# Transposing layer 0's two normalised row tiles by VectorE block transposes and on-chip DMAs instead of TensorE

## The chip, the core and the metric

The kernel runs on one core of a Trainium2 chip. The metric is the device time of one execution in microseconds (us). Three runs of the kernel before gave 2903.96, 2904.14 and 2904.46 us; their median is 2904.14 us.

## The reference

64 independent graphs of 256 nodes with 256 features each go through two graph-attention layers. All arithmetic is 32-bit float.

```python
# layer 0, per graph (src: 256 x 256)
q, k = src @ Wq + bq, src @ Wk + bk                  # 8 heads of 32
attn = softmax(q @ k.T / sqrt(32))
out  = sum over r of (attn * (adj == r)) @ (src @ Wv[r] + bv[r])
x    = layernorm(src + out @ Wo + bo) * g1 + beta1
x    = layernorm(x + gelu(x @ W1 + b1) @ W2 + b2) * g2 + beta2
# layer 1, per graph
q, k, v = x @ Wq, x @ Wk, x @ Wv
e    = leaky_relu(q @ k.T, 0.2), edges with adj == 0 masked out
h    = layernorm(softmax(e) @ v)
y    = layernorm(concat(h, x) @ Wffn.T) + x
```

adj holds 0 and 1 alone, so only r = 0 and r = 1 of layer 0 matter.

## The kernel before, in words

One graph's activations fit in tiles of 128 partitions x 512 floats. "Rows" tiles hold nodes on the partitions (two blocks `t` of 128 nodes, 256 features each), "transposed" tiles hold features on the partitions (two blocks `c` of 128 features, 256 nodes each). A matmul contracts over partitions, so whatever is multiplied by a weight on its features must be in transposed form, while a layer norm, which sums over features, is done in rows form. So a normalised tile of layer 0 has to be transposed twice per graph: once after the first layer norm (`y0` to `y0T`, which feeds the matmuls `ph0`, `ph4`, `ph2`, `ph6` with W1, L665), and once after the second (`y1` to `y1T`, which feeds layer 1's `pq1`, `pk1`, `pv1` and `pwb`).

Each of the two goes like this in the kernel before (L653-654 and L692-693):

1. the rows tile with its residual added is in PSUM (`pwo` at L397, `pw2` at L397); VectorE takes the statistics (`mv0`, L406 to L410), GpSimd the reciprocal root (`rs0`, L415), VectorE writes the normalised rows `y0` to SBUF (L421, two instructions);
2. `transpose` (L364): TensorE transposes four 128x128 blocks of `y0` into the PSUM tile `py0` (L369);
3. `with_gain` (L380): ScalarE reads `py0`, applies gain and shift per feature (now per partition) and writes `y0T` (L385, two instructions).

`y0` is also read by GpSimd, which makes the residual for the next step from it (`r1`, and `x2` from `y1`).

PSUM tiles of the tag `g` (128 x 512 floats) come from four rotating buffers: a new `g` tile takes the buffer of the fourth `g` tile before it, and has to wait until that one's readers are done. `y` tiles have four buffers, `yT` tiles three, score tiles `s` two.

**The order of the work is written out by hand.** `program(g)` makes one graph's operations, each bound to one engine (PE = TensorE, ACT = ScalarE, DVE = VectorE, POOL = GpSimd, SP = the queue that issues DMAs). `in_order` (L45) sorts the operations of all graphs by `50 * graph + STARTS[name]`; every engine executes its own operations in that order, and semaphores between the engines keep the data dependencies. So the numbers of STARTS (L100) are places in a sequence, not times: the value modulo 50 is the place within one round of 50, and the whole part of value / 50 says how many rounds after the graph's own number it comes. One round holds one operation of each name, each for a different graph. The first four and the last four graphs have lists of their own (FIRST, L121, and LAST, L180). A name with `#2` is the second operation that writes this tile: `pwo` is the matmul, `pwo#2` VectorE's addition to it.

The operations around the change, with their engines: `pwo`, `pw2` ... `pw2#8` (PE, L357 and L683), `pwo#2`, `pw2#9` (DVE, L397), `mv0`, `mv1` (DVE), `rs0`, `rs1` (POOL), `y0`, `y1` (DVE), `py0`, `py1` (PE, L369), `y0T`, `y1T` (ACT, L385), then `ph0` ... `ph6` (PE, L665) and `pq1`, `pk1` (PE, L343), whose results ScalarE copies out as `q1`, `k1` (L513). On SP: the loads `xT`, `adj`, `x` (L334) of a later graph and the store `SP:y2` (L752) of an earlier one; four DMAs of 256 KB for each graph.

Of the kernel before, what the change touches and what calls it, by code (L numbers as in the profile page):

```python
# [9 lines left out]
F32 = mybir.dt.float32  # L10
I32 = mybir.dt.int32
AF = mybir.ActivationFunctionType
# [11 lines left out]
P = 128  # L24
D = 256
H, DH = 8, 32
KC = 2
NT = 2
# [16 lines left out]
def in_order(programs, starts, period, first, last):  # L45
# [4 lines left out]
    for g, p in enumerate(programs):  # L50
# [23 lines left out]
    "yT": ([KC, D], F32, 3),  # L74
    "hT": ([8, D], F32, 2),
# [25 lines left out]
    "xT": 47.54, "adj": 54.92, "neg": 55.74, "pq0": 56.97, "q0": 60.25, "pk0": 70.08, "k0": 70.90, "s000": 72.95,  # L101
    "e00/0": 81.15, "m00/1": 81.56, "m00/0": 87.70, "e00/1": 90.98, "pva0": 93.44, "s010": 94.26, "v0/0": 95.08,
    "e01/0": 96.72, "x": 97.13, "m00/1#2": 97.95, "pva1": 100.82, "res": 101.64, "e01/1": 102.05, "es00/1": 102.87,
    "v0/1": 103.28, "es01/0": 104.10, "m00/0#2": 106.56, "m01/1": 107.38, "m01/1#2": 107.79, "m01/0": 108.61,
    "m01/0#2": 109.43, "es00/0": 111.07, "po00": 111.48, "rd00": 112.30, "o0/0": 112.70, "es01/1": 113.11,
    "po01": 114.34, "rd01": 114.75, "o0/1": 115.16, "DVE:po01": 115.57, "DVE:po00": 116.39, "ACT:adj": 118.44,
    "pwo": 118.85, "pwo#2": 119.26, "mv0": 119.67, "rs0": 123.77, "y0": 124.18, "py0": 124.59, "y0T": 125.00,
    "r1": 129.51, "ph0": 131.97, "ph4": 132.79, "hT/0": 134.43, "hT/4": 134.84, "ph2": 135.25, "hT/2": 135.66,
    "ph6": 136.07, "hT/6": 136.48, "r1#2": 138.11, "pw2": 138.52, "pw2#2": 138.93, "pw2#3": 139.34, "pw2#4": 139.75,
    "pw2#5": 140.16, "pw2#6": 140.57, "pw2#7": 141.39, "pw2#8": 141.80, "pw2#9": 142.21, "mv1": 142.62,  # L110
    "rs1": 145.49, "y1": 145.90, "py1": 148.36, "y1T": 148.77, "pk1": 153.69, "pq1": 154.51, "k1": 155.33,
    "q1": 158.20, "s100": 159.02, "e10/0": 159.84, "m10/0": 160.66, "e10/1": 161.89, "x2": 163.52, "m10/1": 163.93,
    "s110": 165.98, "e11/0": 166.80, "m11/1": 167.21, "pv1": 167.62, "v1": 168.03, "m11/0": 170.49,
    "e10/1#2": 171.31, "e11/1": 172.13, "pwb": 172.54, "e10/0#2": 173.36, "e11/0#2": 175.41, "zb": 176.64,
    "e10/1#3": 177.05, "es10/1": 177.46, "e11/1#2": 182.38, "e10/0#3": 183.20, "e11/0#3": 183.61, "es10/0": 184.02,
    "e11/1#3": 186.89, "es11/1": 193.03, "po10": 193.85, "es11/0": 194.67, "po11": 196.31, "rd10": 199.18,
    "DVE:po11": 199.59, "o1/0": 200.00, "DVE:po10": 200.41, "rd11": 201.23, "o1/1": 202.46, "x2#2": 206.15,
    "ph": 221.72, "mv2": 225.82, "rs2": 226.23, "pwa": 227.87, "pwa#2": 228.28, "mv3": 228.69, "rs3": 229.10,
    "y2": 229.92, "y2#2": 230.33, "y2#3": 230.74, "SP:y2": 237.30,
# [3 lines left out]
        -6346.377, -6530.16, -6982.832, -6634.0, -6093.635, -5736.533, -6045.455, -6290.298, -5672.953, -5696.302,  # L123
        -5008.862, -5888.0, -6453.208, -5286.254, -5289.164, -5677.61, -5529.665, -5461.611, -5372.746, -5225.073,
        -6469.019, -6080.346, -6152.781, -6125.275, -4362.988, -5833.733, -5164.614, -4798.404, -4797.673, -4604.086,
        -4447.748, -4217.049, -4504.134, -4458.784, -4528.298, -4512.584, -4486.596, -4386.977, -4471.14, -4517.811,
        -4507.195, -4500.964, -4440.287, -4140.093, -3943.527, -3880.12, -4070.372, -4482.976, -4318.59, -4355.735,
        -3960.397, -4120.247, -4007.041, -4233.453, -3919.755, -3659.796, -3372.614, -3087.747, -3087.745, -3268.679,
        -2967.259, -2926.763, -2863.365, -2782.082, -2781.512, -2755.252, -2748.099, -2686.058, -2632.076, -2707.74,
        -2705.657, -2705.031, -2700.944, -2685.9, -2604.336, -2686.294, -2686.292, -2646.722, -2624.727, -2539.089,  # L130
        -2539.087, -2505.953, -2421.823, -2357.5, -2351.019, -2331.649, -2323.477, -2267.498, -2264.329, -2251.442,
        -2239.549, -2082.718, -1742.488, -2220.232, -2148.049, -2233.172, -2172.786, -1880.195, -1803.811, -1665.215,
        -1633.036, -2121.976, -2044.14, -1964.977, -1619.288, -1541.806, -1429.851, -2083.25, -1979.867, -1976.405,
        -1728.291, -1571.446, -1125.134, -1014.844, -994.266, -1059.277, -1945.625, -1773.239, -1843.378, -1724.266,
        -1604.233, -1188.745, -1683.584, -1843.165, -1482.837, -1349.351, -1250.224, -1002.469, -959.959, -933.061,
        -923.019, -780.327, -701.906, -611.768, -466.222, -464.592, -457.638, -381.397, -381.219, -245.27, -76.323,
        -60.729,
    ],
    [
        -3150.342, -2865.684, -3030.007, -2576.407, -1841.393, -2066.514, -2885.805, -2846.503, -2989.537, -2895.209,  # L140
        -2350.813, -2298.896, -2388.858, -2356.392, -2796.464, -2491.226, -2412.218, -2372.987, -2249.024, -2796.462,
        -2534.009, -2422.489, -2656.667, -2121.572, -1907.235, -1891.659, -1835.387, -2294.698, -2255.475, -2262.772,
        -2094.331, -2029.961, -2282.964, -2245.64, -2060.464, -2214.911, -2003.143, -1885.89, -1885.888, -1851.81,
        -1869.958, -1811.256, -1803.92, -1792.147, -1719.479, -1710.833, -1682.568, -1683.327, -1663.512, -1666.775,
        -1637.889, -1611.072, -1579.957, -1548.682, -1486.084, -1628.459, -1484.026, -1524.627, -1411.414, -1396.412,
        -1365.969, -1301.34, -1237.148, -1230.262, -1226.745, -1225.363, -1184.068, -1160.852, -1147.648, -1122.337,
        -1055.926, -668.081, -116.769, -1038.706, -1013.221, -1016.299, -997.935, -684.505, -533.528, -782.079,
        -585.735, -956.86, -945.562, -934.723, -729.07, -717.444, -487.763, -941.495, -932.268, -913.562, -765.459,
        -487.338, 86.712, 123.903, 138.251, 125.976, -832.305, -692.509, -819.769, -616.081, -456.587, -301.91,
        -623.652, -788.225, -329.295, -155.628, -127.412, 145.769, 188.646, 190.331, 169.782, 216.272, 226.254,  # L150
        229.932, 231.195, 236.668, 236.67, 238.046, 238.048, 267.639, 267.641, 273.454,
    ],
    [
        -2853.381, -1411.162, -2082.948, -1906.438, -455.655, -1016.668, -2267.454, -2048.524, -1765.164, -1744.282,
        -1234.866, -1230.669, -1174.61, -1071.551, -1744.28, -1452.623, -1459.483, -1353.241, -1089.619, -1529.289,
        -1443.514, -1245.603, -1125.376, -993.997, -951.211, -887.78, -955.455, -1234.076, -1105.384, -1194.403,
        -1071.068, -1064.103, -1157.836, -1089.956, -1017.329, -987.068, -974.658, -922.208, -875.651, -914.051,
        -833.048, -713.969, -707.805, -678.162, -644.192, -607.043, -606.639, -557.459, -429.974, -518.499, -481.768,
        -515.933, -464.185, -388.676, -273.434, -511.029, -416.896, -343.734, -251.228, -68.742, -31.021, -12.646,
        4.579, 4.581, 5.811, 5.813, 42.687, 42.689, 47.599, 68.12, 111.978, 136.328, 266.823, 118.18, 121.579,  # L160
        127.571, 145.419, 164.63, 167.189, 170.12, 182.669, 158.219, 158.221, 158.221, 160.93, 170.277, 192.81,
        158.272, 158.699, 167.979, 167.981, 184.986, 196.227, 197.919, 197.921, 196.229, 159.876, 168.344, 161.714,
        182.428, 182.43, 198.755, 171.609, 165.811, 174.875, 196.176, 196.908, 202.935, 209.414, 209.416, 202.937,
        222.627, 226.067, 227.191, 229.099, 229.955, 229.957, 229.959, 230.172, 242.113, 266.825, 267.746,
    ],
    [
        -1715.159, -307.399, -1860.875, -375.405, 68.756, 11.501, -1090.815, -1056.5, -890.959, -788.563, -40.809,
        -6.228, 12.243, 43.409, -699.157, -572.433, -263.057, 88.419, 14.512, -549.182, -172.795, -45.958, 0.679,
        108.906, 110.242, 113.133, 113.314, -14.853, -9.216, 103.608, 103.61, 70.071, 22.889, 13.277, 66.318, 95.567,
        109.714, 115.504, 115.506, 113.587, 119.215, 122.548, 122.55, 122.552, 127.137, 129.396, 129.398, 138.847,  # L170
# [66 lines left out]
def fast_path(nc, tc, a, out, bad):  # L237
# [13 lines left out]
    with ExitStack() as ctx:  # L251
# [63 lines left out]
        def program(g):  # L315
            ops, used = [], {}

            def T(name):
                return at_(g, name)
# [755 lines left out]
```

## Time and profile before

| | |
|---|---|
| time, median of three runs | 2904.14 us |
| time of the profiled execution | 2903.45 us |
| span of its profile | 2901.5 us |
| TensorE (PE) busy | 2863.8 us, 99% |
| GpSimd (POOL) busy | 2008.1 us, 69% |
| VectorE (DVE) busy | 1964.0 us, 68% |
| ScalarE (ACT) busy | 1776.7 us, 61% |
| DMA queue of SP | 7.9% of the 16 DMA engines' time |
| `py` transposes on PE (L369) | 512, 84.8 us busy in total |
| gain and shift on ACT (L385) | 256, 130.4 us busy in total |

The profile is one execution. "Busy" is the time in which at least one instruction of an engine was under way; matmuls are pipelined, so the duration of one is longer than the distance to the next. "SPq" is the instruction queue of SP, and its DMA rows give the time that the issue took, not the transfer. The chain of waits follows the work that ended last back through whatever released each step. The timeline lists the instructions of an engine in order of time: start, duration, what it is, how many of the same kind follow each other.

### The profile page before, as it was taken

What the parts mean: (1) busy time and instruction counts of PE and PEld (TensorE: products, weight loads), DVE (VectorE), ACT (ScalarE), POOL (GpSimd) and SP (SyncE); (2) the same over time, 40 slices, a digit from 0 to 9 for tenths busy, and PEclk for the clock granted to TensorE, in tenths of its full rate; (3) what the DMA queues carried; (4) which work ended last, traced back from release to release, by engine and by line L of the source; (5) the groups of instructions that cost most, each with busy time, mean ns of one, the idle gap of its engine ahead of it and who ended that gap; (6) DMA issues with size and microseconds to landing.
All of it is one profiled execution on the core that took longest, in us unless ns stands there. A gap on an engine that the chain in (4) does not pass through costs nothing.

```text
span 2901.5 us, 53555 instructions
## 1 busy us (share of the span) xinstructions
PE 2863.8 (99%) x21770; PEld 2152.2 (74%) x21770; DVE 1964.0 (68%) x3668; ACT 1776.7 (61%) x3011; POOL 2008.1 (69%) x1542
## 2 busy tenths in 40 slices
PE   7999999999999999999999999999999999999996
PEld 5777777777777777777777777777777777777775
DVE  4676676766766767667667666676676676766765
ACT  4656656666666566566665665666666656666563
POOL 2667667677677676776776766767767667677666
PEclk9999999999999999999999999999999999999998
DMA  3000000000000000000000000000000000011000
GB/s 113 24 29 19 28 17 30 16 30 30 16 30 30 16 30 15 30 30 16 30 30 16 30 22 23 30 16 30 30 15 30 30 16 30 15 34 34 8 23 12
DMA packets 74331, 76.63 MB, mean 26 GB/s; under 512 B 4449, under 2 KB 73569, under 8 KB 74081
## 3 DMA queue, kind: packets, MB, share of 16 engines
q1 hardware_dynamic: 74080, 73.17, 7.9%
q8 instruction: 173, 2.83, 0.4%
q14 instruction: 78, 0.63, 0.1%
HBM read 56.37 MB, written 16.78 MB: 25 GB/s over the span
## 4 chain that ended last, share of the span: by engine, by line
PE 97%; DVE 1%; POOL 1%; issue 1%; DMA 0%; ACT 0%; SPq 0%; DVEq 0%; POOLq 0%
PE ph L665 15%; PE pw L683 15%; PE po L477 12%; PE s L439 9%; PE pq L343 8%; PE pk L343 8%; PE pva L617 7%; PE pv L357 4%; PE pwa L357 4%; PE pwo L357 4%; PE po L482 4%; PE pwb L357 4%; PE py L369 3%; PE ph L369 1%; POOL e L717 0%
## 5 line engine op out<-in xcount | busy, mean ns | idle before, releaser
L717 POOL TENSOR_TENSOR e<-e,m 128x1024 f32<-128x1024 f32 x256 | 600.3, 2354 | 301.5 <-ACT m L713 299.5
L508 POOL TENSOR_TENSOR es<-e 128x512 f32<-128x512 f32 x512 | 647.1, 1275 | 168.2 <-ACT e L455 127.4
L455 ACT ACTIVATE e<-s 128x1024 f32<-128x1024 f32 x256 | 260.1, 1016 | 389.0 <-PE s L439 363.2
L665 PE MATMUL ph<-y0T,w 128*128 128x256 f32 x2048 | 452.9, 379 | 0.0
L683 PE MATMUL pw<-w,hT 128*128 128x256 f32 x2048 | 452.7, 379 | 0.0
L491 DVE RECIPROCAL rd<-po 128x256 f32<-128x256 f32 x256 | 448.4, 1752 | 2.9 <-PE po L482 2.9
L415 POOL TENSOR_TENSOR rs<-ve,neg_half 128x2 f32<-128x2 f32 x256 | 179.2, 700 | 386.0 <-DVE ve L410 380.8
L665 PEld LDWEIGHTS ph<-y0T,w 128*128 128x128 f32 x2048 | 389.0, 190 | 53.4 <-issue 0.7
L683 PEld LDWEIGHTS pw<-w,hT 128*128 128x128 f32 x2048 | 389.2, 190 | 52.8
L464 DVE TENSOR_TENSOR e<-s,neg 128x1024 f32<-128x1024 f32 x256 | 305.9, 1216 | 155.6 <-PE s L439 152.5
L713 ACT ACTIVATE m<-s 128x1024 f32<-128x1024 f32 x256 | 260.9, 1021 | 228.5 <-PE s L439 140.7
L397 DVE TENSOR_TENSOR pw<-pw,r 128x512 f32<-128x512 f32 x64 | 44.8, 700 | 471.8 <-PE pw L683 464.3
L464 DVE TENSOR_TENSOR m<-s,neg 128x1024 f32<-128x1024 f32 x256 | 301.0, 1213 | 37.4 <-ACT e L455 23.5
L439 PE MATMUL s<-q,k 32*128 32x256 f32 x4096 | 294.2, 400 | 1.9 <-DVE m L464 1.1
L477 PE MATMUL po<-e,v 128*32 128x256 f32 x4096 | 275.3, 385 | 6.1 <-ACT v L513 4.0
L455 ACT ACTIVATE e<-e 128x1024 f32<-128x1024 f32 x256 | 268.8, 1054 | 19.9 <-POOL e L717 19.6
L455 ACT ACTIVATE m<-m 128x1024 f32<-128x1024 f32 x256 | 264.0, 1055 | 9.1 <-DVE m L464 9.0
L439 PEld LDWEIGHTS s<-q,k 32*128 32x128 f32 x4096 | 185.4, 184 | 105.6 <-issue 48.1
L617 PE MATMUL pva<-wv,xT 128*128 128x512 f32 x512 | 241.1, 593 | 0.0
L477 PEld LDWEIGHTS po<-e,v 128*32 128x32 f32 x4096 | 114.9, 110 | 148.3 <-issue 84.6
L672 ACT ACTIVATE hT<-ph,cols 128x256 f32<-128x256 f32 x512 | 196.2, 478 | 11.0 <-PE ph L665 10.2
L385 ACT ACTIVATE y0T<-py,cols 128x256 f32<-128x256 f32 x128 | 65.2, 559 | 182.4 <-PE py L369 182.3
(90 smaller groups left out, 4688.3 us busy)
## 6 DMA issues: line engine op xcount, KB each, us to landing
xT<-xT_dram SPq DMA_DIRECT2D x64, 256.0 KB, 3.0
adj<-adjT_dram SPq DMA_DIRECT2D x64, 256.0 KB, 3.6
x<-x_dram SPq DMA_DIRECT2D x64, 256.0 KB, 2.8
out_dram<-y SPq DMA_DIRECT2D x64, 256.0 KB, 2.2
w<-L_gnn_W_dram SPq DMA_DIRECT2D x2, 1024.0 KB, 10.1
rows<-rows_dram SPq DMA_DIRECT2D x1, 896.0 KB, 8.2
wv<-L_gnn_Wv_dram SPq DMA_DIRECT2D x3, 256.0 KB, 3.2
wk<-L_gnn_Wk_dram SPq DMA_DIRECT2D x2, 256.0 KB, 6.9
```

The source lines that it names most:

```text
L343: nc.tensor.matmul(pt[:, o, :], lhsT=w[:, c, o * P : (o + 1) * P], rhs=s[:, c, :], start=(c == 0), stop=(c == KC - 1),)
L357: nc.tensor.matmul(pt[:, t, :], lhsT=T(s)[:, c, t * P : (t + 1) * P], rhs=w, start=(n == 0), stop=(n == len(parts) - 1),)
L439: nc.tensor.matmul(s[j // 2][:, j % 2, c, :], lhsT=kT[r, hg, c * P : (c + 1) * P], rhs=qT[r, hg, :], start=True, stop=True,)
L455: nc.scalar.activation(T(dst)[:, j], s, AF.Exp, scale=scale, **kw)
L464: lambda: nc.vector.tensor_tensor(T(dst)[:, j], T(src), T("neg")[:, None].to_broadcast([P, 2, NT, D]), ALU.add),
L477: nc.tensor.matmul(po[j * DH : (j + 1) * DH, 0, :], lhsT=v(c, j), rhs=T(e)[:, j, c, :], start=(n == 0 and c == 0), stop=(n == len(parts) - ...
L491: op("DVE", [po], [f"{rd}:rd"], lambda: nc.vector.reciprocal(T(rd), T(po)[:, 1, :]))
L508: lambda: on.tensor_tensor(T(dst)[:, j], T(e)[:, j, 0, :], T(e)[:, j, 1, :], ALU.add),
L617: nc.tensor.matmul(pv.rearrange("p r d -> p (r d)"), lhsT=s[:, c, t * P : (t + 1) * P], rhs=wv0[:, c].rearrange("p r d -> p (r d)"), start ...
L665: nc.tensor.matmul(ph[:, i, :], lhsT=w1[:, c, (f + i) * P : (f + i + 1) * P], rhs=s[:, c, :], start=(c == 0), stop=(c == KC - 1),)
L683: nc.tensor.matmul(T("pw2")[:, t, :], lhsT=T("hT")[:, f + i, t * P : (t + 1) * P], rhs=w2[:, f + i, :], start=(f + i == 0), stop=(f + i == ...
L717: nc.gpsimd.tensor_tensor(T(f"e1{hg}")[:, j], T(f"e1{hg}")[:, j], T(f"m1{hg}")[:, j], ALU.add)
```

## The change

`transpose` is no longer called for `y0` and `y1`, and the PSUM tiles `py0` and `py1` are gone. In their place `turned` does the transposition in two operations: one VectorE instruction transposes every 32x32 block of the rows tile within its own 32 partitions and writes the result to a new SBUF tile `y0b` (tag `yb`, two buffers), and 16 DMAs on SP, each of 16 KB in runs of 128 bytes, bring the blocks to the partitions where they belong in `y0T`. ScalarE then applies gain and shift to `y0T` in place, reading SBUF instead of PSUM. The order of the operations is a new one in all three tables.

```diff
 TAGS:
     "yT": ([KC, D], F32, 3),
+    "yb": ([KC, NT, P], F32, 2),
...
+            def turned(src, dst):
+                blocks = f"{src}b"
+                def emit_blocks():
+                    nc.vector.transpose(
+                        out=T(blocks), in_=T(src).rearrange("p t (c f) -> p c t f", c=KC)
+                    )
+                def emit_places():
+                    for a in range(4):
+                        for b in range(4):
+                            nc.sync.dma_start(
+                                out=T(dst)[32 * b : 32 * b + 32].rearrange("p c (t n) -> p c t n", t=NT)[
+                                    :, :, :, 32 * a : 32 * a + 32
+                                ],
+                                in_=T(blocks)[32 * a : 32 * a + 32, :, :, 32 * b : 32 * b + 32],
+                            )
+                op("DVE", [src], [f"{blocks}:yb"], emit_blocks)
+                op("SP", [blocks], [f"{dst}:yT"], emit_places)
-            def with_gain(src, dst, gain, shift):
+            def with_gain(name, gain, shift):
...
-                            T(name)[:, c, :], T(src)[:, c, :], AF.Identity,
+                            T(name)[:, c, :], T(name)[:, c, :], AF.Identity,
...
-            transpose("y0", "py0")
-            with_gain("py0", "y0T:yT", g10c, be10c)
+            turned("y0", "y0T")
+            with_gain("y0T", g10c, be10c)
...
-            transpose("y1", "py1")
-            with_gain("py1", "y1T:yT", g20c, be20c)
+            turned("y1", "y1T")
+            with_gain("y1T", g20c, be20c)
```

The new STARTS (FIRST and LAST are replaced by new lists of the same kind). `y0T` and `y1T` are now the 16 DMAs on SP, `y0T#2` and `y1T#2` ScalarE's gain and shift:

```diff
+    "xT": 30.24, "adj": 35.48, "pk0": 35.89, "k0": 36.29, "x": 40.32, "neg": 40.73, "pq0": 41.13, "q0": 43.15,
+    "s010": 43.55, "e01/0": 44.35, "pva0": 45.16, "m01/1": 45.56, "v0/0": 45.97, "e01/1": 46.77, "m01/0": 47.98,
+    "pva1": 48.39, "v0/1": 49.19, "s000": 52.02, "m01/1#2": 52.42, "res": 53.23, "e00/1": 54.03, "m00/0": 56.85,
+    "es00/1": 57.66, "m00/0#2": 58.47, "e00/0": 58.87, "es01/0": 59.68, "m00/1": 62.10, "m00/1#2": 63.71,
+    "m01/0#2": 65.73, "es00/0": 66.13, "po00": 67.34, "es01/1": 70.16, "po01": 70.56, "rd01": 70.97, "rd00": 72.58,
+    "DVE:po01": 72.98, "DVE:po00": 73.79, "o0/0": 76.21, "o0/1": 79.84, "pwo": 86.69, "pwo#2": 87.50, "mv0": 87.90,
+    "rs0": 89.52, "y0": 89.92, "y0b": 93.95, "r1": 100.81, "y0T": 103.63, "y0T#2": 105.24, "ACT:adj": 109.27,
+    "r1#2": 112.50, "ph0": 112.90, "ph4": 113.31, "ph2": 116.53, "hT/2": 118.15, "hT/0": 118.55, "hT/4": 121.37,
+    "ph6": 124.60, "hT/6": 125.00, "pw2": 127.02, "pw2#2": 127.82, "pw2#3": 128.23, "pw2#4": 128.63,
+    "pw2#5": 130.65, "pw2#6": 131.05, "pw2#7": 131.45, "pw2#8": 131.85, "pw2#9": 132.26, "mv1": 132.66,
+    "rs1": 133.87, "y1": 134.27, "y1b": 137.10, "y1T": 144.76, "y1T#2": 147.18, "pq1": 152.82, "pk1": 156.05,
+    "k1": 157.26, "q1": 158.06, "x2": 160.08, "s110": 166.94, "e11/1": 167.74, "e11/0": 168.95, "m11/1": 169.35,
+    "m11/0": 169.76, "e11/1#2": 172.18, "s100": 173.39, "e10/0": 174.19, "e11/1#3": 175.81, "e10/1": 176.61,
+    "m10/0": 179.03, "e10/0#2": 179.44, "m10/1": 183.06, "e10/1#2": 183.47, "e10/1#3": 184.68, "e11/0#2": 185.08,
+    "pwb": 188.31, "e10/0#3": 188.71, "zb": 189.11, "es10/1": 191.53, "pv1": 192.34, "e11/0#3": 192.74,
+    "v1": 196.37, "es10/0": 197.58, "es11/0": 198.79, "po10": 199.60, "es11/1": 200.00, "po11": 200.40,
+    "rd10": 201.21, "DVE:po11": 201.61, "rd11": 204.44, "o1/0": 204.84, "DVE:po10": 205.65, "o1/1": 206.45,
+    "ph": 210.48, "pwa": 210.89, "mv2": 211.29, "rs2": 211.69, "pwa#2": 214.11, "mv3": 214.52, "rs3": 214.92,
+    "y2": 215.32, "x2#2": 221.77, "y2#2": 225.40, "y2#3": 227.42, "SP:y2": 241.94,
```

Sorted modulo 50, TensorE's round in the order before is `pva1 pk1 pq1 pq0 s100 po00 po01 s110 pv1 pwo pk0 ph pwb s000 py0 pwa ph0 ph4 ph2 ph6 pw2 ... pw2#8 pva0 po10 s010 po11 py1`, and SP's is `adj SP:y2 x xT`. TensorE's round in the new order is `po11 s000 pq1 pk1 ph pwa ph0 ph4 ph2 s110 po00 po01 s100 ph6 pw2 ... pw2#8 pk0 pwo pwb pq0 pv1 s010 pva0 pva1 po10`, and SP's round is `y0T xT adj x SP:y2 y1T`.

## Prediction

> **What bounds the kernel now.** I read the head of the page first, then the busy times of one stretch in the middle, then TensorE's timeline in that stretch.
>
> ```profile
> span 2901.5 us, 53555 instructions
> PE 2863.8 (99%) x21770; PEld 2152.2 (74%) x21770; DVE 1964.0 (68%) x3668; ACT 1776.7 (61%) x3011; POOL 2008.1 (69%) x1542
> ```
>
> ```profile
> 1000.00:1044.50 44.50, 44.50 (x342) 33.52 (x341) 30.56 (x58) 27.64 (x48) 31.39 (x25) 1.00 0.08 25
> ```
>
> The second line covers one round: window, length, then busy time of PE, PE's weight loads, DVE, ACT, POOL, then the granted clock (1.00). SP's stores come 44.5 us apart, so one graph takes 44.5 us, and PE is busy in all of it. No other engine is busy for more than 31.4 us. TensorE's work is the limit in the middle, and what leaves it shortens the round, unless something else then ends last.
>
> ```profile
> 1015.87 1.15 PE L439 MATMUL s<-q,k 32*128 32x256 f32 x16
> 1016.95 0.66 PE L369 MATMUL py<-ident,y 128*128 128x128 f32 x4
> 1017.44 1.89 PE L357 MATMUL pwa<-wf,o 128*128 128x256 f32 x8
> ...
> 1032.98 1.88 PE L617 MATMUL pva<-wv,xT 128*128 128x512 f32 x4
> ...
> 1038.73 0.66 PE L369 MATMUL py<-ident,y 128*128 128x128 f32 x4
> 1039.22 0.59 PE L617 MATMUL pva<-wv,xT 128*128 128x512 f32 x1
> ```
>
> Read the starts, not the durations: the work behind a `py` starts 0.49 us after it (1017.44 - 1016.95, 1039.22 - 1038.73). That is a `py`'s price on PE.
>
> **Removed.** Two `py` a graph, 0.98 us, times 64: 62.7 us off PE. (The Trainium skill, "TensorE: Matmul & The Clock Gate", Part 4, gives about 275 ns for a transpose in a kernel's context. The duration in the trace agrees, a median of 273 ns, but four follow each other within 0.49 us, so 512 x 275 ns = 141 us would overstate the gain.) The round would fall to 44.5 - 0.98 = 43.5 us. Two PSUM tiles of tag `g` per graph go as well; PE waits for nothing in the round now, so that gains nothing.
>
> **Added on DVE.** 128 block transposes of 128x512 floats; the trace has none. Nearest row: an addition of that shape, 0.68 to 0.70 us (L397). The ends are 0.41 us (a 128x256 operation, L494) and 3.5 us (twice the reciprocal's 1.75 us for 128x256). I take 0.68: DVE goes from 30.6 to 31.9 us a round and stays hidden behind PE, except in the latency below.
>
> **Changed on ACT.** The gain reads SBUF instead of PSUM. ACT's exponentials of 128x1024 take 1054 ns from SBUF and 1016 ns from PSUM, so at 4% more it is nothing on an engine that is 62% busy.
>
> **Added on SP: 32 DMAs a graph**, beside the four there are. What matters is the distance between two issues.
>
> ```profile
> 0.73 0.40 SPq L520 DMA_DIRECT2D cols<-cols_dram  x1
> 1.18 0.42 SPq L520 DMA_DIRECT2D wv<-L_gnn_Wv_dram  x1
> ```
>
> ```profile
> 1026.30 0.38 SPq L752 DMA_DIRECT2D out_dram<-y  x1
> 1026.73 0.46 SPq L334 DMA_DIRECT2D x<-x_dram  x1
> 1027.28 0.46 SPq L334 DMA_DIRECT2D xT<-xT_dram  x1
> 1027.83 0.42 SPq L334 DMA_DIRECT2D adj<-adjT_dram  x1
> ```
>
> `cols` is the only one of like size (12 KB in 128 runs): the next begins 0.45 us later. After the 256 KB store it is 0.43, between the 256 KB loads 0.55. The shortest issue is 0.37 us, so 0.42 with a gap of 0.05. I take **0.45**, from the nearest row; the ends are 0.42 and 0.55. Time to landing:
>
> ```profile
> out_dram<-y SPq DMA_DIRECT2D x64, 256.0 KB, 2.2
> cols<-cols_dram SPq DMA_DIRECT2D x1, 12.0 KB, 1.7
> ```
>
> I take 1.7 us for 16 KB; 2.2 is the other end. SP's busy time, 36 x 0.45 = 16 us of 43.5, is no limit, and 34 MB more (128 x 256 KB) in short runs, beside today's 73, falls on DMA engines that are 7.9% busy. The transfers of the loads are ordered before their use by a whole stretch of the round, so the loads that are now queued behind 16 or 32 issues still come in time. (A rule that speaks against the change: the Trainium skill, "DMA: Bandwidth & Descriptors", Rules for kernel authors, wants small transfers joined, since under 64 KB one pays mostly overhead, and puts the fixed part of one DMA near 2 us. If it were paid one after the other, 32 x 2 = 64 us a graph would make the kernel over 4000 us; the trace shows issues 0.45 us apart and landings of 1.7 us, so the fixed part overlaps.)
>
> **The added wait, and what it must fit into.** A `py` was ready half a microsecond after `y`; now there are 16 DMAs between. In the new order, between the end of a graph's `pw2#8` and the next `ph0` (of the following graph), PE has, by the starts in the timeline: `pk0 pwo pwb pq0 pq1 pk1 pwa`, 7 x 1.73; `pv1` 1.82; `s010` and `s000`, 2 x 1.08; `pva0` 1.72; `pva1` 1.81; `po10` 1.32; `po11` 1.43; `ph` 0.44. Together **22.8 us** of cover. The other 20.6 us, from `ph0` to `pw2#8`, make up the round.
>
> Against it stands a chain, because SP's order puts both transpositions one behind the other: `y1T` (place 44.76 of a round; its data hangs on `pw2#8`), then at once `y0T` of the following graph (place 3.63 of the next round), which `ph0` needs. How long VectorE's part takes can be read at the end of the chain of waits, where nothing else is in its way:
>
> ```profile
> 2854.01 0.71 DVE pw L397
> ...
> 2854.74 0.76 DVE st L406 x2
> 2855.50 0.22 DVE mv L408 x2
> 2855.72 0.20 DVE ve L410 x2
> ...
> 2855.98 0.71 POOL rs L415
> ...
> 2856.72 1.01 DVE y L421 x2
> ```
>
> From `pw` to the end of `y`: 3.72 us. The chain: 0.30 until VectorE sees `pw2#8` (PE's next work starts at 1032.98, VectorE at 1033.28); 3.72; 0.3, an estimate, for `rs1` behind a 2.35 us addition of `e` on POOL; 0.68 for `y1b`; 0.3, an estimate, for hand-overs and buffer waits: SP starts at 5.3 us. The 32nd issue starts 31 x 0.45 = 13.95 later, at 19.25, and has landed at 20.95 (`y0b` is ready near 10, long before SP reaches it). ACT: gain 1.02 (two instructions in the timeline), then `k1` and `q1`, 1.07, which the order queues behind the gain and which `ph0` needs, since its PSUM buffer is the one of `pq1`, four `g` tiles earlier. Hand-over 0.1: **23.15 us against 22.8**. `ph0` comes 0.34 us late in each round, 63 x 0.34 = 21 us. (`y1T` alone lands at 13.8, gain until 14.9; `pq1` has 17.2 us of cover: hidden.)
>
> **Start and end.** In the last 40 us PE is idle a good part of the time (14.58 of 20 us busy, then 6.98 of 21.5), and the chain runs through `py` and gain of the last graph's `y1`: 1.2 us there become 0.68 + 15 x 0.45 + 1.7 + 1.0 = 10.1. One such exposure, about 8 us; the other three at the two ends (first graph's, last graph's `y0`) I take as covered by other graphs' scores.
>
> **Sum**, against the profiled execution's own 2903.45 us (span 2901.5; 0.7 below the median of 2904.14): 2903.45 - 62.7 + 21 + 8 = 2869.8; **2870 us**.
>
> **Rivals.**
>
> 1. *All hidden.* At 0.42 us an issue the chain is 22.2 us and fits; the wait of 21 us is gone: 2849 us. With a covered end, 2841. For it: three issues in the trace at 0.37 to 0.38. Together with the forecast's own neighbourhood (up to 2885) 0.50; between there and 2898 us another 0.07.
> 2. *Slower, by SP's issue distance.* Each 0.01 us per issue costs 31 x 0.01 x 63 = 20 us once the chain is longer than its cover. From 0.467 us on the whole gain is lost; at the loads' 0.55 the chain is 26.25, 3.44 us over in each round, 217 us: 2903.45 - 62.7 + 217 + 8 = 3066 us. Halfway, at 0.50, 2968. Against it: those rows move 256 KB each, 16 times as much, and each of the later ones stands behind another. For it: the break-even is only 0.02 us off, and a landing of 2.2 us would add 32 us more. 0.37, of which up to 3010 us 0.22, beyond 0.15; into the latter fall a block transpose at the upper end (2.8 us more in the chain, 178 us: 3048) and DMAs that wait for each other to land: 32 x 1.7 = 54 us is longer than a round, 64 x 54 = some 3500 us.
> 3. *It does not take work off the limit*: wait and gain cancel, within 0.2% (about what a measurement of this kernel can tell from no change), 2898 to 2910: 0.06.
>
> Range: 2838 (all hidden, a `py` slot 0.05 larger) to 3010, which leaves out about 0.17. The likeliest case's own range is 2840 to 2890. Faster 0.57, same 0.06, slower 0.37.
>
> **What would show it.** In the profile after: no `py` on PE; the round between SP's stores 43.5 us if hidden, 43.9 as forecast, 46.9 in the slow case; a gap on PE ahead of `ph0` put down to ACT (`q1` or the gain), and ACT's gain waiting for a DMA; 16 issues on SP 0.45 us apart. I am wrong if PE is as full as before and yet the round isn't shorter, if the gap on PE is ahead of `pq1`, or if the issues wait for landings.

## The result, and the profile after

The changed kernel takes **3392.35 us** (median of four runs, 3387.91 to 3397.56); beside it on the same chip the kernel before took 2904.30 us. The ratio is 1.1681, 95% interval 1.1661 to 1.1701: 488 us slower, where 34 us faster was forecast. The profiled execution took 3387.91 us, span 3386.1 us.

The head of the page after (busy time, share of the span, instructions), and the chain of waits by engine:

```profile
span 3386.1 us, 56035 instructions
PE 2964.1 (88%) x21258; PEld 2190.3 (65%) x21258; DVE 2041.6 (60%) x3796; ACT 1789.9 (53%) x3011; POOL 2007.2 (59%) x1542
PE 60%; SPq 28%; DMA 4%; issue 3%; ACT 2%; DVE 1%; POOL 1%; ACTq 0%; DVEq 0%; POOLq 0%
```

The 512 `py` matmuls are gone (21770 to 21258), yet PE's busy time has risen by 100 us and its share fallen from 99% to 88%. SP's queue, which computes nothing, now holds 28% of the chain that ended last; by line all of it is L394, the 32 DMAs of a graph. PE both stands idle and works slower. The timelines of one round show where. SP first (start, duration, what, how many in a row):

```profile
1409.75 0.38 SPq L774 DMA_DIRECT2D out_dram<-y  x1
1421.33 10.74 SPq L394 DMA_DIRECT2D y1T<-y1b  x16
1432.19 10.97 SPq L394 DMA_DIRECT2D y0T<-y0b  x16
1443.20 0.59 SPq L336 DMA_DIRECT2D xT<-xT_dram  x1
```

Each burst of 16 takes almost 11 us, and `y0T` starts where `y1T` ends. ACT's two gains in the same round (in brackets: idle time ahead, and what ended it), then PE around them:

```profile
1434.55 1.09 ACT L407 ACTIVATE y1T<-y1T,cols 128x256 f32<-128x256 f32 x2 [5.49 <-DMA y0T<-y0b]
...
1444.87 1.09 ACT L407 ACTIVATE y0T<-y0T,cols 128x256 f32<-128x256 f32 x2 [7.29 <-DMA y0T<-y0b]
1445.87 0.56 ACT L535 COPY k<-pk 128x512 f32<-128x512 f32 x1
```

```profile
1435.20 2.05 PE L345 MATMUL pq<-y1T,wq 128*128 128x256 f32 x8 [1.35 <-DMA y0T<-y0b]
...
1439.26 1.89 PE L359 MATMUL pwa<-wf,o 128*128 128x256 f32 x8
1446.48 8.38 PE L687 MATMUL ph<-y0T,w 128*128 128x256 f32 x24 [5.34 <-ACT k L535]
1454.79 1.15 PE L461 MATMUL s<-q,k 32*128 32x256 f32 x16
```

(The brackets at 1434.55 and 1435.20 name `y0T`, but by the trace `y1T`'s last DMA landed at 1434.29 and `y0T`'s first at 1434.74, behind the gain's start: what the gain of `y1T` waited for, and `pq1` behind it, is `y1T`.) PE has nothing to do for 5.34 us ahead of `ph0`: ACT waits for the DMA, makes the gain, copies `k1`, and only then may `ph0` start. And the 24 `ph` matmuls behind the gap take 8.31 us until the next start (1454.79 - 1446.48), where 24 of them took 5.27 in rounds without a gap. The stretches of that round, with window, length, busy PE, PEld, DVE, ACT, POOL, granted clock, DMA share and GB/s, say why:

```profile
1416.55:1439.26 22.71, 21.36 (x150) 15.20 (x149) 17.04 (x32) 10.55 (x20) 15.63 (x13) 1.00 0.13 18
1439.26:1446.48 7.22, 1.89 (x10) 1.33 (x8) 5.45 (x17) 1.61 (x4) 4.71 (x5) 0.94 0.25 56
1446.48:1449.00 2.52, 2.52 (x6) 2.07 (x7) 0.00 (x0) 2.52 (x5) 0.05 (x1) 0.50 0.00 0
1449.00:1452.00 3.00, 3.00 (x8) 2.37 (x8) 0.00 (x0) 2.98 (x5) 3.00 (x3) 0.50 0.45 107
1452.00:1455.00 3.00, 3.00 (x16) 2.35 (x19) 0.00 (x0) 0.87 (x2) 0.67 (x1) 0.93 0.19 68
```

Behind the gap the granted clock (the share of TensorE's full clock) is 0.50 for 5.9 us: the 5.52 us up to 1452.00 and, by the mean of 0.93 in the last stretch, 0.4 more. Half of 5.9 us is 2.95, nearly all of the 3.04 us by which these 24 matmuls take longer. (The Trainium skill, "TensorE: Matmul & The Clock Gate", Part 1, says that an idle window of about 3.4 us brings the clock to 4/8. The 0.50 behind a gap of 5.34 us agrees.) PE is "busy" in those stretches: that is why its busy time rose.

So one round, 44.5 us before, is 52.0 us now (mean distance of SP's stores over 41 rounds, 50.8 to 53.6). Means over 48 rounds give its parts: 43.5 of work, 5.4 of gap ahead of `ph0`, 0.6 ahead of `pq1`, 2.2 of slow clock in `ph` (7.5 instead of 5.34 busy); 0.3 is left over. 60 rounds of 7.5 us more are 450 of the 484 us between the two profiled executions; of the other 34, 8.5 lie ahead of SP's first store (150.5 us from the start, 142.0 before), the rest among the first and the last graphs; I did not follow them further.

### The profile page after: what moved, and what is told of

Its sections match the earlier page's. It is cut to its first block, busy times and chain, and to the rows that moved or that the text cites. A ratio compares the mean times of both kernels' runs of the same rounds, so it can differ in the third digit from the quotient of the medians.

```text
span 3386.1 us, 56035 instructions
## 1 busy us (share of the span) xinstructions
PE 2964.1 (88%) x21258; PEld 2190.3 (65%) x21258; DVE 2041.6 (60%) x3796; ACT 1789.9 (53%) x3011; POOL 2007.2 (59%) x1542
## 4 chain that ended last, share of the span: by engine, by line
PE 60%; SPq 28%; DMA 4%; issue 3%; ACT 2%; DVE 1%; POOL 1%; ACTq 0%; DVEq 0%; POOLq 0%
SPq L394 28%; PE ph L687 17%; PE pw L705 13%; PE po L499 8%; PE s L461 5%; PE pk L345 3%; PE pwo L359 3%; PE pwb L359 3%; PE pva L639 3%; PE po L504 2%; DMA y0T<-y0b 2%; DMA xT<-xT_dram 2%; PE pq L345 2%; PE pv L359 1%; ACT y0T L407 1%
## 5 line engine op out<-in xcount | busy, mean ns | idle before, releaser
L530 POOL TENSOR_TENSOR es<-e 128x512 f32<-128x512 f32 x512 | 638.1, 1271 | 562.4 <-ACT e L477 554.6
L687 PE MATMUL ph<-y0T,w 128*128 128x256 f32 x2048 | 592.8, 454 | 319.9 <-ACT k L535 172.6
L687 PEld LDWEIGHTS ph<-y0T,w 128*128 128x128 f32 x2048 | 462.5, 232 | 446.8 <-ACT k L535 314.3
L513 DVE RECIPROCAL rd<-po 128x256 f32<-128x256 f32 x256 | 440.6, 1739 | 179.8 <-PE po L504 179.7
L486 DVE TENSOR_TENSOR m<-s,neg 128x1024 f32<-128x1024 f32 x256 | 311.0, 1217 | 92.4 <-PE s L461 70.2
L694 ACT ACTIVATE hT<-ph,cols 128x256 f32<-128x256 f32 x512 | 206.9, 473 | 264.4 <-PE ph L687 264.3
L407 ACT ACTIVATE y0T<-y0T,cols 128x256 f32<-128x256 f32 x128 | 69.8, 592 | 444.8 <-DMA y0T<-y0b 444.8
L407 ACT ACTIVATE y1T<-y1T,cols 128x256 f32<-128x256 f32 x128 | 69.9, 593 | 309.9 <-DMA y1T<-y1b 277.3
```

Source lines behind the costliest of these rows:

```text
L486: lambda: nc.vector.tensor_tensor(T(dst)[:, j], T(src), T("neg")[:, None].to_broadcast([P, 2, NT, D]), ALU.add),
L513: op("DVE", [po], [f"{rd}:rd"], lambda: nc.vector.reciprocal(T(rd), T(po)[:, 1, :]))
L530: lambda: on.tensor_tensor(T(dst)[:, j], T(e)[:, j, 0, :], T(e)[:, j, 1, :], ALU.add),
L687: nc.tensor.matmul(ph[:, i, :], lhsT=w1[:, c, (f + i) * P : (f + i + 1) * P], rhs=s[:, c, :], start=(c == 0), stop=(c == KC - 1),)
```

## The experiments

**Is it the transposition's latency or the new order?** `order_only` keeps the new order and puts both transpositions back on TensorE.

```diff
-            turned("y0", "y0T")
-            with_gain("y0T", g10c, be10c)
+            turned_pe("y0", "y0T")                    # 4 PE transposes into PSUM
+            with_gain_pe("y0b", "y0T", g10c, be10c)   # gain from PSUM, as before
     (the same for y1; "y1b" moved from 137.10 to 139.50)
```

> The changed kernel with both transpositions back on TensorE (gain read from PSUM again), in the new order; y1's transposition stands two places later on TensorE than VectorE's one did. Theory (SP's issue distance, 0.65 us a DMA, makes ph0 late): nothing is left on SP, TensorE is full again, 44.5 us a round, 2900 to 2930 us. Rival (the new order itself, e.g. k1 and q1 queued behind the gain, costs the time): a gap ahead of ph0 stays and the time is above 3150 us.

Measured 2974.51 us (2968.14 to 2978.78), ratio 1.0240 [1.0223, 1.0257]. PE in `order_only`:

```profile
1443.24 1.89 PE L359 MATMUL pwa<-wf,o 128*128 128x256 f32 x8
1444.96 5.34 PE L709 MATMUL ph<-y0T,w 128*128 128x256 f32 x24
```

Rounds of 44.9 us, no gap ahead of `ph0`. The order alone costs some 70 us, more than I expected, only 24 us (60 x 0.4) of it in the middle, the rest among the first and the last graphs. The other 418 us come with the DMAs.

**Is it the number of DMAs?** `eight` halves it. Which 32x32 block goes where is left out (the blocks stay in their partitions), so only its time counts.

```diff
-                    for a in range(4):
+                    for a in range(2):
                         for b in range(4):
...
-                                    :, :, :, 32 * a : 32 * a + 32
+                                    :, :, :, 64 * a : 64 * a + 64
...
-                                in_=T(blocks)[32 * a : 32 * a + 32, :, :, 32 * b : 32 * b + 32],
+                                in_=T(blocks)[32 * b : 32 * b + 32, :, :, 64 * a : 64 * a + 64],
```

> 8 DMAs of 32 KB in runs of 256 bytes in place of 16 of 16 KB; the blocks stay in their own 32 partitions, so the exchange of blocks between partition groups is left out. Bytes are the same. Theory (number of issues times 0.65 us): the chain is 4.8 + 15 x 0.66 + 2.1 + 1.9 = 18.7 us against 22.8 of cover, no gap ahead of ph0, round 43.5 us, 2845 to 2870 us. Rival (bytes or landing times on the DMA engines): 3300 to 3400 us.

Measured 2867.04 us (2862.96 to 2868.05), ratio 0.9872 [0.9855, 0.9888], as expected. The SP and PE timelines of `eight`:

```profile
1417.29 5.11 SPq L394 DMA_DIRECT2D y1T<-y1b  x8
1422.51 6.04 SPq L394 DMA_DIRECT2D y0T<-y0b  x8
```

```profile
1433.73 1.89 PE L359 MATMUL pwa<-wf,o 128*128 128x256 f32 x8
1435.46 5.34 PE L687 MATMUL ph<-y0T,w 128*128 128x256 f32 x24
```

Twice the bytes in half as many DMAs, and one issue costs the same. The bursts halve, `ph0` follows `pwa` without a gap, the round is 43.6 us: just what the removal of the `py` promised. The same volume does no harm, and neither does VectorE's part.

**One transposition of the two.** `y0_dma` does only `y0` by blocks and DMAs, `y1_dma` only `y1`; the other is on TensorE as in `order_only`.

```diff
 y0_dma:
-            turned("y1", "y1T")
-            with_gain("y1T", g20c, be20c)
+            turned_pe("y1", "y1T")
+            with_gain_pe("y1b", "y1T", g20c, be20c)
     (y1_dma: the same for y0)
```

> Only y0 goes by block transposes and DMAs; y1 is transposed on TensorE again (two places later than its block transpose stood), in the new order. Theory (the two transpositions queue on SP, each 16 x 0.66 = 10.6 us): y0b is ready 9.1 us after pw2#8, its DMAs are through at 9.1 + 15 x 0.66 + 2.1 = 21.1, gain and k1 until 23.0, against 22.8 + 0.5 of cover: hidden, round 44.0 to 44.5 us, 2900 to 2960 us with the ends as in order_only. Rival (each transposition by itself costs half of the loss, by its landing or its place in the order): 3130 to 3200 us.

> Only y1 goes by block transposes and DMAs; y0 is transposed on TensorE again, in the new order. Theory: y1T's DMAs start 4.8 us after pw2#8, are through at 4.8 + 15 x 0.66 + 2.1 = 16.8, gain until 18.1, against 17.2 + 0.5 of cover ahead of pq1: 0.4 us late at most, round 44.0 to 44.9 us, 2890 to 2960 us. Rival (each transposition by itself costs half of the loss): 3130 to 3200 us.

Measured 2934.66 us (ratio 1.0102 [1.0085, 1.0119], rounds 44.0) and 2953.31 us (1.0172 [1.0155, 1.0189], rounds 44.5). Neither has a gap ahead of `ph0` (`y1_dma` has 0.4 us a round ahead of `pq1` and `pk1`). Both times lie in the ranges expected. Each is even some 20 to 40 us faster than `order_only`; it takes both in one chain to lose 418 us.

**What makes an issue take 0.60 us?** `plain` moves runs of 512 bytes instead of 128, `wide16` uses all 128 partitions in each of the 16 DMAs (and also loads `x` in four quarters, to see DMAs of other kinds behind each other). Both leave out the right places of the blocks.

```diff
 plain:
-                                out=T(dst)[32 * b : 32 * b + 32].rearrange("p c (t n) -> p c t n", t=NT)[
-                                    :, :, :, 32 * a : 32 * a + 32
-                                ],
-                                in_=T(blocks)[32 * a : 32 * a + 32, :, :, 32 * b : 32 * b + 32],
+                                out=T(dst)[32 * b : 32 * b + 32].rearrange("p c (t n) -> p (c t) n", t=NT)[:, a],
+                                in_=T(blocks)[32 * a : 32 * a + 32].rearrange("p c t n -> p (c t) n")[:, b],
 wide16:
...
+                    for j in range(16):
+                        nc.sync.dma_start(
+                            out=T(dst).rearrange("p c n -> p (c n)")[:, 32 * j : 32 * j + 32],
+                            in_=T(blocks).rearrange("p c t n -> p (c t n)")[:, 32 * j : 32 * j + 32],
+                        )
...
+                for b in range(4):
+                    nc.sync.dma_start(out=T("x")[32 * b : 32 * b + 32], in_=ap[32 * b : 32 * b + 32])
```

> 16 DMAs of 16 KB between groups of 32 partitions as in the change, but each moves one run of 512 bytes per partition in place of four of 128; the places within a row are left out, so the transposed tile is in a wrong order. If the 0.60 us of an issue come from the pattern (four short runs a partition, 128 descriptors): issue 0.37 to 0.45, chain 4.8 + 31 x 0.45 + 2.1 + 1.9 = 22.7, 2845 to 2900 us. If they come from a DMA between two partition groups of SBUF whatever its runs: issue 0.60, 3390 us.

> 16 DMAs of 16 KB within SBUF per transposition as in the change, but each over all 128 partitions (one run of 128 bytes a partition, same partition to same partition; the exchange of blocks is left out), and the load of x from HBM split into four DMAs of 32 partitions. It measures the issue: if SBUF to SBUF makes it 0.6 us, y0T and y1T stay at 0.60 and the x loads at 0.37 to 0.46, round 50 to 53 us, 3250 to 3400 us. If 32 partitions make it 0.6 us, y0T and y1T fall to 0.37 to 0.46, the four x loads rise to 0.6, and the kernel is at 2850 to 2900 us.

Measured 3332.16 us (1.1471 [1.1452, 1.1490]) and 3336.06 us (two runs; 1.1486 [1.1463, 1.1509]), both with rounds of 51.2 us and a gap ahead of `ph0` of 5.0 and 5.2 us in the mean. (The 60 us by which they are faster than the change I did not follow.) Neither the runs nor the partitions make the issue shorter than 0.59 us in the median. In `wide16` the first DMA of `y1T`'s burst takes 0.47 us and the next ones 0.60, from the second on. The quarter loads of `x`, 64 KB in runs of 1 KB, take 0.43 us in the median, though four of them stand one behind the other, 0.47 to 0.51 us apart. So standing behind another DMA does not by itself make an issue 0.60 us long; runs of more than 512 bytes or pieces of more than 32 KB were not tried in the bursts.

So perhaps it is the source in SBUF. `hbm16` reads the same 16 KB pieces from `x` in HBM; the transposed rows are left out.

```diff
-                                in_=T(blocks)[32 * a : 32 * a + 32, :, :, 32 * b : 32 * b + 32],
+                                in_=x_d[g].rearrange("(t p) (c q n) -> p c t q n", p=P, c=KC, n=32)[
+                                    32 * a : 32 * a + 32, :, :, b
+                                ],
```

> As the changed kernel, but each of the 32 DMAs of a graph reads its 16 KB (runs of 128 B, same destinations) from x in HBM instead of from y0b or y1b; the transposed rows are thereby left out, and the DMAs no longer wait for VectorE. Only the issue time and the distance of the issues are asked for. If it is the source in SBUF that makes an issue take 0.60 us, these take 0.42 to 0.46 us as the HBM loads of the kernel before, and both bursts 7 us each. If it is the burst of many DMAs with short runs, they take 0.60 us again, 0.64 us apart, and the round stays at 50 us or more.

The instructions of that line in `hbm16` (durations in ns: least, median, most), and SP's timeline:

```profile
L394 SPq DMA_DIRECT2D y0T<-x_dram x1024: 578/602/1773, 20.3 to 2771.1; - x171
L394 SPq DMA_DIRECT2D y1T<-x_dram x1024: 578/602/1800, 33.2 to 2808.2; - x171
```

```profile
1409.06 0.38 SPq L776 DMA_DIRECT2D out_dram<-y  x1
1409.54 10.28 SPq L394 DMA_DIRECT2D y1T<-x_dram  x16
1419.92 10.94 SPq L394 DMA_DIRECT2D y0T<-x_dram  x16
```

The source is not it: 0.602 us again. But this kernel takes 2864.16 us (two runs; ratio 0.9860 [0.9831, 0.9889]), with rounds of 43.6, against what I expected of slow issues. The same 32 issues, just as slow, cost nothing here, since no DMA waits for VectorE: the first burst starts 0.48 us behind the store's start, where after the change it started 11.58 us behind it. The slow issue is dear only as part of the chain from `pw2#8` to `ph0`.

**The chain, or the slow clock?** `fill` keeps the chain and keeps PE busy in the gap, by doing `pwa` five times over.

```diff
-                    for t in range(NT):
+                    for t in [t for _ in range(times) for t in range(NT)]:
...
-            linear([("o1", c, wf[:, c, :]) for c in range(KC)], "pwa", ["c_wf"])
+            linear([("o1", c, wf[:, c, :]) for c in range(KC)], "pwa", ["c_wf"], 5)
```

> The changed kernel with pwa's eight matmuls done five times over (same result), 6.9 us of work for TensorE in the gap ahead of ph0. Theory (the gap also costs clock: ph0 to ph2 take 8.3 us in place of 5.2 after it): they take 5.2 us again, round 53.0 to 50.2 us, 3190 to 3230 us. Rival (the granted clock plays no part, the round is set by the chain alone): 3390 us or more.

Measured 3384.16 us (1.1649 [1.1630, 1.1668]): hardly faster than the change, and a miss. The time is not told apart from the rival's 3390 us; the duration of `ph` is what decides. PE in `fill`:

```profile
1434.93 8.80 PE L359 MATMUL pwa<-wf,o 128*128 128x256 f32 x40
1443.57 5.34 PE L687 MATMUL ph<-y0T,w 128*128 128x256 f32 x24
```

The clock effect is confirmed: with no gap the `ph` matmuls are back at 5.34 (5.40 in the mean of 50 rounds, 7.5 after the change), at a mean clock of 0.989. But the filler is 6.9 us of PE's time in place of a gap of 5.4, and 43.5 + 6.9 = 50.4, with 0.7 us a round of other gaps (0.6 ahead of `pq1`), is the round that it has, 51.1. I had taken one long round, with 3.1 us of clock loss, for all, and had not counted the filler where there is no gap to fill.

**Half of `y0T` on another queue.** `two_queues` issues eight of `y0T`'s DMAs from ACT's queue.

```diff
...
+                if split:
+                    op("ACT", [blocks], [f"{dst}:yT"], lambda: emit_places(range(2), nc.scalar))
+                    op("SP", [blocks], [dst], lambda: emit_places(range(2, 4)))
...
+    "y0T": 96.90, "y0T#2": 103.63, "y0T#3": 105.24     (ACT's half, SP's half, gain)
```

> The whole change, but half of the y0T DMAs (8 of 16) are issued from ScalarE's queue, ahead of the gain of y1T, at a place where ScalarE stood idle for 5.5 us; the other half stays on SP's behind the 16 of y1T. Theory (the two bursts queue one behind the other on SP, and it is the issuing that takes the time): 8 x 0.65 = 5.2 us leave the chain in front of ph0, so of the 7 us of gap about 2 are left, the round falls from 52.1 to 45-46 us and the kernel to 2980-3040 us. Rival (the DMAs inside SBUF hinder each other after the issue, and the issue is only held back by that): two queues share the same transfers, each then takes about twice as long to issue one (over 1.0 us), and the round stays above 50 us, the kernel above 3300 us.

Measured 3443.87 us (1.1862 [1.1844, 1.1880]): neither theory. Start, duration and number on SP and then on ACT:

```profile
1441.46 10.26 SPq L394 DMA_DIRECT2D y1T<-y1b  x16
1451.83 6.21 SPq L394 DMA_DIRECT2D y0T<-y0b  x8
```

```profile
1453.72 6.83 ACTq L394 DMA_DIRECT2D y0T<-y0b  x8
1460.66 1.09 ACT L411 ACTIVATE y1T<-y1T,cols 128x256 f32<-128x256 f32 x2 [11.47 <-DMA xT<-xT_dram]
```

ACT was free at 1449, but its first issue came 2.0 us after SP's last of `y1T`. The chain of waits shows ACT's issues released by the landing of SP's DMAs, and the trace shows by what: all DMAs of this kernel, on both queues, take their turn on eight semaphores that tell of landings, and none is issued before the DMA ahead of it on the same semaphore has landed. ACT's first issue, at 1453.72, has the semaphore of SP's last but one of `y1T`, which landed at 1453.70. 264 of ACT's 512 issues in the execution start within 0.06 us behind such a landing of one of SP's. (With all DMAs on SP, as after the change, none comes closer than 1.85 us, so this wait is not what makes the single queue slow.) The gain of `y1T` stood behind ACT's issues in its queue and came some 6.5 us late. So the gap has moved: PE waits 7.2 us ahead of `pq1` in the mean, and not at all ahead of `ph0`. The run does not test what it was made for. The time is the rival's (over 3300 us, rounds of 53.1), but its mechanism is not there: an issue takes 0.60 us on SP and 0.61 on ACT in the median, not over 1.0. The 16 DMAs of this round took 8.7 us, 0.78 us an issue on SP and 0.85 on ACT, with those waits inside; between issues that did not have to wait, while both queues were at work, the median distance is 0.645 us on SP and 0.65 on ACT (14 cases).

**Only the cover.** `replan` keeps the whole change, with its 32 slow issues, and changes the order alone.

```
 PE round, after:  po11 s000 pq1 pk1 ph pwa ph0 ph4 ph2 s110 po00 po01 s100 ph6 pw2 ... pw2#8 pk0 pwo pwb pq0 pv1 s010 pva0 pva1 po10
-PE's round as above, FIRST and LAST with four lists each
+PE: ph po01 pwa s110 po00 ph2 ph6 ph0 ph4 pw2 ... pw2#8 pwo s100 pwb pk0 pq0 pv1 s010 po11 pva1 pva0 po10 s000 pk1 pq1
+FIRST with one list, LAST = []
```

> The whole change with another order of the steady state, and one plain order for the first and the last graphs. In it the 32 DMAs keep their measured 0.6-0.65 us each, but y1T's burst stands ahead of y0T's with more of TensorE's work behind each: ph0 comes after po01, pwa, s110, po00, and pk1, pq1 come at the round's end. Theory (only the cover was too short for a chain of 30 us; the DMAs as such cost nothing on TensorE): no gap ahead of ph0 and pq1, TensorE's round at its own work, 43.5 to 43.8 us, ends as in before or 20 us worse, 2870-2920 us. Rival (32 DMAs of the SBUF cost beyond SP's time, by slower reads or by held-back loads): round above 45 us, 2980 us or more.

Measured 2984.87 us (2980.52 to 2985.57), ratio 1.0278 [1.0264, 1.0292]. SP and PE in `replan`:

```profile
1435.07 10.25 SPq L261 DMA_DIRECT2D y1T<-y1b  x16
1446.26 10.80 SPq L261 DMA_DIRECT2D y0T<-y0b  x16
```

```profile
1414.92 1.05 PE L366 MATMUL po<-m,v 128*32 128x256 f32 x16
1415.78 0.61 PE L371 MATMUL po<-es,ones 128*32 128x256 f32 x8
1416.33 7.17 PE L554 MATMUL ph<-y0T,w 128*128 128x256 f32 x32
```

The bursts are as long as after the change, and no gap is left: the round is 44.9 us instead of 52.0, and 407 us are back, with all 32 DMAs in place. That is the theory's main point. The numbers were still missed, and the time is in the rival's range (2980 us or more; its round of above 45 is just not reached). The round is 1.3 us longer than in `eight`. 0.6 of it is in `s`, one of whose four groups takes 1.68 us in place of 1.08 in nearly every round; the rest is up to 0.23 in each of several other groups of matmuls. What makes them longer was not followed, so by this run alone a cost of the 32 DMAs beyond the chain, of up to 1.3 us a round, is not excluded. Against it speak `eight`, with the same bytes inside SBUF, and `hbm16`, with 32 DMAs of the same size: both have rounds of 43.6. The plain order costs more at the start: SP's first store comes at 201.2 us, 59 us later than before. `replan` does not beat the kernel before; of the kernels that compute everything, none here does.

## Why the prediction was wrong

The frame held; one term of the sum failed, and one cost was missing. Step by step, from the end of `pw2#8` (1416.55 in the round above) to `ph0` (1446.48):

| step | forecast | measured |
|---|---|---|
| SP starts with `y1T` | 5.3 us | 4.8 |
| from the first to the 32nd issue | 31 x 0.45 = 13.95 | 21.23 = 31 x 0.685 |
| the 32nd, from its start until landed | 1.7 | 2.05 |
| gain, copy, hand-over | 2.19 | 1.87 |
| chain | 23.15 | 29.93 |
| work on PE beside it | 22.8 | 23.24 |
| PE late in this round | 0.34 | 6.69 = 1.35 ahead of `pq1` + 5.34 ahead of `ph0` |

**The step that failed** is "I take **0.45**, from the nearest row; the ends are 0.42 and 0.55." `cols` was one DMA with others of other kinds around it, and the 0.55 came from loads of 256 KB. Sixteen or 32 small DMAs back to back cost 0.60 us of issue and 0.04 between, and now and then one takes up to 1.8 us, which made 0.685 in this round and 0.668 in the mean of all. That is above both ends, so even the range could not hold the time. Of the 6.35 us by which the round above is later than forecast, 7.28 are this term; the others together take off 0.93. The trace of before had nearer rows than the three that were used, at its start, where SP issues 21 DMAs in 20 us:

```profile
17.76 0.66 SPq L334 DMA_DIRECT2D adj<-adjT_dram  x1
18.46 0.66 SPq L334 DMA_DIRECT2D x<-x_dram  x1
19.17 0.66 SPq L334 DMA_DIRECT2D xT<-xT_dram  x1
```

They are loads of 256 KB, but stand 0.70 us apart, and single issues among the 21 take up to 2.33 us. Why they take longer there than in the middle no run shows, but the upper end of 0.55 left them out. I had named this rival (slower, by SP's issue distance), with its place and break-even of 0.467, and had given it only a chance of 0.37 and an end at 0.55.

**Put at nothing in the sum**: what a gap does to PE behind it. The clock at 0.50 adds 2.2 us to each round, 63 x 2.2 = 139 us in all; the page's row has `ph` at 592.8 us busy after the change, 452.9 before. In the middle of the kernel before, PE never stood idle, and my text counted a gap at its length alone. But the last 40 us of that trace, whose busy times the forecast quotes, had the rows (columns as above; the third number from the end is the granted clock):

```profile
2860.00:2880.00 20.00, 14.58 (x101) 9.71 (x99) 13.08 (x26) 9.88 (x15) 13.63 (x8) 0.86 0.00 1
2880.00:2901.50 21.50, 6.98 (x34) 3.95 (x34) 10.98 (x28) 0.02 (x1) 9.78 (x10) 0.58 0.08 27
```

```profile
2875.16 1.94 PE L477 MATMUL po<-e,v 128*32 128x256 f32 x16 [3.97 <-ACT v L513]
2876.86 1.08 PE L482 MATMUL po<-es,ones 128*32 128x256 f32 x8
```

Behind a gap of 3.97 us these 16 matmuls take 1.70 us until the next start, where they took 0.89 in the middle (1034.79 to 1035.68), and the granted clock of the two stretches is 0.86 and 0.58. With the means of the rounds after the change, 6.0 us late instead of 0.34 is 63 x 5.7 = 359 us, and the clock 139: together 498 of the 518 us between the forecast of 2869.8 and the profiled execution's 3387.91.

The other steps:

- PE's slots: right. 43.6 us a round in `eight` and `hbm16`, 43.5 forecast.
- VectorE's block transpose: 0.71 us (0.68 taken), and hidden. VectorE's timeline after:

```profile
1420.56 0.71 DVE L387 STREAM_TRANSPOSE y1b<-y 128x512 f32<-128x512 f32 x1
```

- That `ph0` needs both copies, `k1` and `q1` (1.07 us): wrong, only `k1` held it back. `ph0` started 0.05 us behind the end of `k1`'s copy and 0.43 ahead of the end of `q1`'s.
- The gain from SBUF: 592 ns against 559, 6% more (4% taken), no matter.
- "The loads that are now queued behind 16 or 32 issues still come in time": right; `hbm16` and `eight` have no gap with them.
- "`pq1` has 17.2 us of cover: hidden": wrong, for the same reason. From the first to the 16th issue it was 10.15 us instead of 15 x 0.45 = 6.75, and `pq1` was 0.6 us late in the mean.
- Start and end, 8 us: too small. `eight`, where all is hidden in the middle, took 2862.96 us in its profiled execution, 22 us above 2903.45 - 62.7; `order_only` loses some 45 us outside its middle rounds. That the lists of the first and last graphs suit other latencies is likely, but not tested.
- DMAs that wait for each other to land (3500 us): no; on one queue landings of 1.8 us overlap, the bursts are issue after issue.
- What would show it: the gap ahead of `ph0`, put down to ACT's copy, with ACT's gain waiting for a DMA, was there as written. 46.9 us for the slow case became 52.0.

What makes an issue in such a burst cost 0.60 us stays open. Shown is what it is not: the length of the runs (128 to 512 bytes), the size (16 or 32 KB), the number of partitions (32 or 128), or the source (SBUF or HBM). Longer runs, larger pieces and another destination than SBUF were not tried.

## What to carry to other kernels

When a change puts many DMAs into a chain, take the distance of their issues from a row where as many of the same kind stand back to back; if there is none in the middle, look at the start and the end as well, where the trace of before had both rows that this forecast lacked, and let the upper end lie above them. Multiply by the whole queue: two bursts that are harmless apart make one long chain when the order puts them behind each other, and then the order, or half as many DMAs, takes the loss away, not the engine (`replan` and `eight`; no kernel here that computes everything became faster than the one before). And a gap on TensorE of some 5 us costs not only its length, but also the slow clock behind it, here 2.2 us a round.

## What the runs showed of the hardware

- SP needs 0.60 us for each issue in a burst of small DMAs, the next one comes 0.645 later in the median, for 16 KB as for 32 KB, from SBUF as from HBM; a 256 KB load right behind a burst takes 0.59 as well, the first of `y1T`'s burst 0.47 to 0.59, and the loads and stores of the middle, elsewhere, 0.37 to 0.50.
- Two queues side by side keep that distance, 0.645 us on SP and 0.65 on ACT, where nothing else holds an issue; in `two_queues` the eight semaphores that both share held 264 of ACT's 512 issues.
- After an idle 5.34 us, the granted clock was 0.50 for 5.9 us, and 24 matmuls took 8.31 instead of 5.27 us. After the idle 1.35 us of the same round it was still 1.00.
